# Token numbers of a mixture-of-experts layer copied out of the row buffers after the last convolution, and seven row buffers instead of eight

## The chip, the core and the metric

The kernel runs on one core of a Trainium2 chip. Its engines are PE (TensorE, matrix products), ACT (ScalarE, activations and copies out of PSUM), DVE (VectorE, elementwise work and reductions), POOL (GpSimd; here it issues the indirect DMAs above all) and SP (SyncE; here it only issues DMAs). The metric is the device time of one execution in microseconds (us). The median of three runs of the kernel before is 3093.45 us.

## The reference, cut to what matters

Input is x of 8 x 56 x 56 x 256 in float32, that is 25088 tokens of 256 channels. A convolution block of 32 parallel paths is followed by an attention step with a linear kernel and by a mixture of eight experts, each token taking the two that its router likes best. The last part is the one that the change touches:

```python
logits = tokens.astype(jnp.float32) @ router_w.astype(jnp.float32).T
probs = jax.nn.softmax(logits, axis=-1)
rw, re = jax.lax.top_k(probs, TOP_K)
...
for e in range(E):
    h = jax.nn.gelu(tokens @ w1[e] + b1[e], approximate=False)
    y = h @ w2[e] + b2[e]
    out = out + combine[:, e:e + 1] * y
```

The sum over the experts has only two terms a token that aren't zero. The kernel computes those two and adds each to the output row of its token.

## The kernel before, in words

**Slots.** The main loop runs over slots `s`. The input is cut into S = 56 chunks of 448 tokens (seven an image), and in slot `s` the convolution of chunk `s` runs together with the attention of chunk `s - 8` and with tiles of the experts' work whose tokens are already known. After slot 56 no convolution is left; slots 57 to 64 hold the last attention and routing and more tiles, and behind the loop come the remaining tiles.

**Routing.** For each group of chunks `route_steps` picks the two experts of every token, counts its place in each expert's list, and writes into the token's row three numbers behind its 256 channels: the two weights and, in column C + 2, the number of the token as an integer. POOL then scatters the rows into DRAM (`regions`, L1163), one region for the first choice (k = 0) and one for the second (k = 1), sorted by expert. When some chunks of an image are done, `plan_steps` (L1189) makes a plan of further tiles: for each, the first row in the region and the expert. There are 17 such plans, each of n tiles with k = 0 and then n tiles with k = 1; n tiles of one k are called a block here. All in all there are 210 tiles of 256 rows. The last plan holds tiles 176 to 192 (k = 0) and 193 to 209 (k = 1). Of each of its two blocks the first two tiles are surely full; the other fifteen can hold only part of their rows.

**One tile.** The steps of a tile `i` are spread over rounds. `moe_steps` (L1473) puts into round `n`:

1. `tile_in(n)`: PE turns the rows of tile n (L1375), ACT copies them out as `eT` (L1379); ahead of the next step one `tile_add`
2. `tile_mid(n - 1, 0)`: PE's first product with the expert's weights (L1415), ACT's gelu (L1419); one `tile_add`
3. `tile_mid(n - 1, 1)`, then `take_rows(n + 2)`: SP loads the 256 rows of tile n + 2 (L1354)
4. `tile_out(n - 2, 0)`: PE's second product (L1431, L1435), ACT's scaling by the router's weight into `y` (L1439); then `take_weights(n + 1)`: SP loads that tile's weights (L1364)
5. `tile_out(n - 2, 1)`

`tile_add` (L1444) issues on POOL an indirect DMA (L1453) that adds one half of y, 128 rows, to the output rows of its tokens. A tile has two such scatters. They take the token numbers as their index. `ordered_sum` (L1461) makes the scatters of a block wait until all those of the block before have landed, since two blocks can add to the same output rows; inside a block no row occurs twice.

**Buffers.** Row tiles (tag `rows`, 128 x 2 x 259 float32) have eight buffers, weights (`w`) four, `y` four of 128 x 2 x 256. A row buffer is read by PE (the turning), by ACT in `tile_out` (the router's weight, column C + k) and, in most tiles, by the scatters, whose index is the column C + 2 of the buffer itself. It is free when all these are done. In the thirty tiles that can be partly filled the index is already a buffer of its own: DVE makes it (L1386, L1387) from the column and from the number of the first valid row. These have 12 buffers of tag `index`.

**Order.** PE, ACT and DVE run their instructions in the order in which the program names them; the steps of a slot are placed by hand with the numbers in `places`. The instructions of SP and POOL are ordered by the compiler, from program order and from which buffers are free. [...] SP carries the loads of rows and weights, and also the loads and stores of the convolution and the attention (`tT` L958, `X` L959, the store of X L1034).

**A flag.** `apart` is an empty list until slot 57 and holds one element from then on (L1600). Up to now it only decides whether the two halves of a tile share one PSUM bank or have one each (`bank_of`). By the numbers in `places["after"]` and the plan, tile 129 is the first whose `tile_in` runs in slot 57.

**The start.** `empty_rows` (L1339) is called once in each of slots 1 to 8; it fills a buffer of tag `rows` with zeros and stores it into both regions.

Of the kernel before, what the change touches and what calls it, by code (L numbers as in the profile page):

```python
# [8 lines left out]
F32 = mybir.dt.float32  # L9
BF16 = mybir.dt.bfloat16  # L10
I32 = mybir.dt.int32
# [14 lines left out]
def kernel(  # L26
# [24 lines left out]
    nc = tc.nc  # L51
    B, N, C = x.shape
# [6 lines left out]
    P = 128  # L59
# [397 lines left out]
    slots = ctx.enter_context(tc.tile_pool(name="slots", bufs=4))  # L457
# [43 lines left out]
    ROW = C + 3  # L501
# [6 lines left out]
    def paced(ins):  # L508

        tc.add_manual_dep(ins, pace[0].name, SYNC, reason="spread over the slot")  # L510
        return ins
# [92 lines left out]
    def unordered(ins, group, keep=()):  # L604

        tc.declare_no_dep(ins, group=group, keep=keep, reason="other rows")
# [447 lines left out]
    def filled(b, ins):  # L1054
        unordered(ins, "rows")
        unordered(ins, "tiles")
        tc.add_to_no_dep_group("rows", ins)
        before.setdefault(b, []).append(ins)
# [266 lines left out]
    def entry(i, j, most):  # L1325

        place, own, k, partial, b = slot_of[i]
        loads, (value,) = nc.values_load_multi_w_load_instructions(
            place[0:1, j : j + 1], engines=[mybir.EngineType.SP],
            min_val=0, max_val=most,  # L1330
            skip_runtime_bounds_check_because="a tile's row and expert, made on the chip",
        )
        if b not in landed:
            landed.add(b)
            for ins in before[b]:
                tc.add_manual_dep(loads[0].ins, ins.name, SYNC, reason="rows of the tiles")
        return value

    def empty_rows(e):  # L1339
        pad = slots.tile([P, 2, ROW], F32, tag="rows", name=f"pad_{e}", bufs=8)  # L1340
        nc.gpsimd.memset(pad, 0.0)
        for k in range(2):
            ins = nc.sync.dma_start(
                out=regions[k][e * CAPR : e * CAPR + TR, :].rearrange("(h p) c -> p h c", p=P),
                in_=pad,
            ).ins
            paced(ins)
            filled(0, ins)

    def take_rows(i):  # L1350
        row = entry(i, 0, E * CAPR - TR)
        z = slots.tile([P, 2, ROW], F32, tag="rows", name=f"rows_{i}", bufs=8)
        region = regions[slot_of[i][2]]
        ins = nc.sync.dma_start(  # L1354
            out=z, in_=region[bass.ds(row, TR), :].rearrange("(h p) c -> p h c", p=P)
        ).ins
        unordered(ins, "rows")
        tc.add_to_no_dep_group("tiles", ins)
        got[i] = z
# [9 lines left out]
    def tile_in(i):  # L1369
        z = got.pop(i)  # L1370
        k = slot_of[i][2]
        tp = ps_mm.tile([P, NF, TR], F32, tag="mm", name=f"te_{i}")
        for f in range(NF):
            for h in range(2):
                nc.tensor.transpose(  # L1375
                    tp[:, f, h * P : (h + 1) * P], z[:, h, f * P : (f + 1) * P], ident
                )
        eT = work.tile([P, NF, TR], F32, tag="eT", name=f"eT_{i}")
        nc.scalar.copy(eT, tp)  # L1379
        g = z[:, :, C + k]  # L1380
        index = [z[:, h, C + 2 :].bitcast(I32) for h in range(2)]
        low = slot_of[i][3]
        if low is not None:
            index = slots.tile([P, 2], I32, tag="index", name=f"index_{i}", bufs=12)
            past = slots.tile([P, 2], I32, tag="past", name=f"past_{i}", bufs=2)
            nc.vector.tensor_scalar(past, pos, low, float(1 << 30), ALU.is_lt, ALU.mult)  # L1386
            nc.vector.tensor_tensor(  # L1387
                index, z[:, :, C + 2].bitcast(I32), past, ALU.bitwise_or
            )
            index = [index[:, h : h + 1] for h in range(2)]  # L1390
        turned[i] = (eT, g, index)

    apart = []
# [79 lines left out]
    def moe_steps(first, last):  # L1473


        steps = []

        def some(fn, i, *args):
            if 0 <= i < N_ALL:
                fn(i, *args)  # L1480

        for n in range(first, last):
            steps.append((0.5, lambda n=n: (some(tile_in, n), tile_add())))
            steps.append((1.0, lambda n=n: (some(tile_mid, n - 1, 0), tile_add())))
            steps.append((1.0, lambda n=n: (some(tile_mid, n - 1, 1), some(take_rows, n + 2))))
            steps.append((1.0, lambda n=n: (some(tile_out, n - 2, 0), some(take_weights, n + 1))))
            steps.append((1.0, lambda n=n: some(tile_out, n - 2, 1)))
        return steps
# [53 lines left out]
    for s in range(S + A + 1):  # L1542
# [53 lines left out]
        if 1 <= s <= E:  # L1596
            work_of.append((0.5, 0.5, [(0.0, lambda: copy_weights(s - 1))]))
            work_of.append((0.8, 0.8, [(0.0, lambda: empty_rows(s - 1))]))
# [65 lines left out]
```

## Time and profile before

| What | Value |
|---|---|
| median of three runs | 3093.45 us |
| lowest and highest run | 3087.57 and 3095.67 us |
| the profiled execution's own time | 3092.02 us |
| its span (first to last instruction) | 3090.3 us |
| mean granted clock of PE | 0.972 |
| PE busy | 2875.4 us, 93% |
| DVE busy | 2124.4 us, 69% |
| ACT busy | 1920.2 us, 62% |
| POOL busy | 1800.1 us, 58% |
| scatters that add y to the output (L1453, index in the row buffer) | 360, 1575 ns mean |
| scatters of rows into the regions (L1163) | 448, 957 ns mean |
| loads of rows, of weights | 210 each |

How to read it: busy times are sums over the whole span, and the stages differ. The convolution fills PE until slot 56; the expert tiles that the change touches run late, so what matters is read from the last 400 us, in the timelines of single engines and in busy times by stage. In a timeline each line has the start and the duration in us, the engine and line, the operation and its tiles, the number of merged instructions, and in brackets the idle time of the engine before it and what ended that. In a table of waits the three numbers are the total in us, how often, and the longest. In busy times by stage come first the stage and its length, then the busy time (and count) of PE, of PE's weight loads, of DVE, ACT and POOL, the granted clock, the DMA engines' busy share and GB/s. A wait for several semaphores is put down to the one that came last by the profile; an engine named there that had long been done was not what was waited for.

### The profile page before, as it was taken

The page shows a single profiled execution, that of the slowest core. Times are in us where ns is not written, and L with a number is a line of the kernel's source. Part 1 is how long each engine was busy: PE and PEld are TensorE (multiplying, and loading weights), DVE is VectorE, ACT ScalarE, POOL GpSimd, SP SyncE. Part 2 cuts the span into 40 slices and gives each one's busy share as a digit, 9 for nine tenths or more (in the row PEclk, how much of TensorE's full clock was granted, in tenths as well). Part 3 has the DMA queues.
Part 4 walks back from the last instruction along what each step waited for, and adds up shares of the span by engine and source line. Part 5 has one row for each costly group of instructions (what it writes and reads, how often), then busy time and mean ns, then how long its engine had stood idle before and what let it go on. Part 6 is the DMA issues. An engine that isn't in the chain of part 4 may idle for free.

```text
span 3090.3 us, 53454 instructions
## 1 busy us (share of the span) xinstructions
PE 2875.4 (93%) x16677; PEld 1645.2 (53%) x16677; DVE 2124.4 (69%) x5532; ACT 1920.2 (62%) x3859; POOL 1800.1 (58%) x1333
## 2 busy tenths in 40 slices
PE   7999898888999999999999999999999997997798
PEld 3334443433455555555555555555555554776687
DVE  6877778788777777787777777787778784544000
ACT  4666566556666666667766666666666764554355
POOL 2332344445465765756766666576664556676677
PEclk8999999889999999999999999999999999998899
DMA  3534344436456777677776776767766666998897
GB/s 101 151 118 129 115 141 134 129 98 198 140 158 185 186 193 188 177 198 190 193 193 164 197 197 171 200 168 199 198 171 175 184 169 157 228 254 201 201 236 172
DMA packets 321708, 537.53 MB, mean 174 GB/s; under 512 B 40192, under 2 KB 231824, under 8 KB 321424
## 3 DMA queue, kind: packets, MB, share of 16 engines
q1 hardware_dynamic: 238464, 429.89, 45.6%
q0 software_dynamic: 82368, 103.47, 18.6%
q8 instruction: 133, 2.18, 0.3%
q14 instruction: 151, 1.24, 0.1%
q10 hardware_dynamic: 592, 0.76, 0.1%
HBM read 248.01 MB, written 192.55 MB: 143 GB/s over the span
## 4 chain that ended last, share of the span: by engine, by line
PE 72%; DVE 8%; ACT 6%; POOL 5%; DMA 5%; issue 4%; SPq 0%; ACTq 0%; POOLq 0%; DVEq 0%
PE c L660 14%; PE su L681 13%; PE ph L1415 11%; PE py L1435 9%; PE at L983 7%; PE kv L829 3%; PE c L324 3%; ACT r L665 3%; POOL hsd L793 3%; PE te L1375 3%; PE c L288 2%; DVE r L668 2%; PE py L1431 2%; DMA w<-Wd 2%; DMA out_dram<-y,rows 2%
## 5 line engine op out<-in xcount | busy, mean ns | idle before, releaser
L668 DVE SCALAR_TENSOR_TENSOR r<-c,nb,r 128x448 f32<-128x448 f32 x1792 | 1128.3, 677 | 401.2 <-ACT r L665 395.5
L665 ACT ACTIVATE r<-c,b3t 128x448 f32<-128x448 f32 x1792 | 1036.6, 634 | 342.6 <-PE c L660 338.1
L1453 POOL DMA_INDIRECT out_dram<-y,rows x360 | 567.0, 1575 | 415.6 <-ACT y L1439 262.8
L660 PE MATMUL c<-hl,W3hl 64*128 64x448 f32 x3584 | 684.9, 427 | 32.5 <-ACT r L665 18.7
L1163 POOL DMA_INDIRECT regions<-pay,rrowi x448 | 428.5, 957 | 308.9 <-PE c L660 172.8
L660 PEld LDWEIGHTS c<-hl,W3hl 64*128 64x128 f32 x3584 | 324.3, 188 | 490.6 <-issue 207.7
L681 PE MATMUL su<-r,gather 128*32 128x448 f32 x3584 | 532.2, 564 | 36.3 <-DVE r L668 32.5
L1415 PE MATMUL ph<-eT,w 128*128 128x256 f32 x1680 | 454.5, 402 | 40.2 <-DMA w<-Wd 24.0
L1439 ACT ACTIVATE y<-py,rows 128x256 f32<-128x256 f32 x420 | 196.9, 473 | 442.0 <-PE py L1435 364.9
L1435 PE MATMUL py<-w,hT 128*128 128x256 f32 x1680 | 432.8, 382 | 0.0
L1415 PEld LDWEIGHTS ph<-eT,w 128*128 128x128 f32 x1680 | 301.2, 194 | 173.0 <-issue 45.8
L793 POOL TENSOR_TENSOR hsd<-hsd,half 112x36 f32<-112x36 f32 x49 | 302.7, 6178 | 88.0 <-DVE hsd L791 84.1
L754 POOL TENSOR_TENSOR norm<-t,hmean 112x512 f32<-112x512 f32 x112 | 115.5, 1057 | 361.0 <-DVE hmean L743 220.9
L1419 ACT ACTIVATE hT<-ph,w 128x256 f32<-128x256 f32 x420 | 198.1, 476 | 187.7 <-PE ph L1415 130.9
L1435 PEld LDWEIGHTS py<-w,hT 128*128 128x128 f32 x1680 | 292.1, 192 | 29.3
L983 PE MATMUL at<-tab,tT 128*112 128x272 f32 x896 | 258.2, 411 | 7.1 <-ACT r L665 5.9
L681 PEld LDWEIGHTS su<-r,gather 128*32 128x32 f32 x3584 | 97.2, 109 | 218.7 <-issue 101.7
L1431 PE MATMUL py<-b2hl,own 128*128 128x256 f32 x420 | 182.2, 434 | 11.6 <-ACT lg L991 7.8
L983 PEld LDWEIGHTS at<-tab,tT 128*112 128x112 f32 x896 | 148.3, 179 | 81.5 <-issue 27.7
L987 DVE SCALAR_TENSOR_TENSOR X<-at,rs,X 112x256 f32<-112x256 f32 x224 | 107.0, 478 | 107.2 <-PE at L983 106.6
L1431 PEld LDWEIGHTS py<-b2hl,own 128*128 128x128 f32 x420 | 80.5, 192 | 141.8 <-issue 48.0
L324 PE MATMUL c<-R,W2t 96*32 96x448 f32 x1344 | 149.3, 546 | 0.1
(263 smaller groups left out, 3063.1 us busy)
## 6 DMA issues: line engine op xcount, KB each, us to landing
w<-Wd SPq DMA_DIRECT2D x210, 513.0 KB
rows<-regions SPq DMA_DIRECT2D x210, 259.0 KB
xi<-in_x_dram SPq DMA_DIRECT2D x56, 448.0 KB
hl<-hi SPq DMA_DIRECT2D x112, 224.0 KB
tTs<-xT SPq DMA_DIRECT2D x56, 448.0 KB
ts<-t SPq DMA_DIRECT2D x56, 448.0 KB
tT<-tTs SPq DMA_DIRECT2D x56, 448.0 KB
X<-ts SPq DMA_DIRECT2D x56, 448.0 KB
```

Of the source, the lines that this page charges most:

```text
L324: nc.tensor.matmul(ps[0][32 * g : 32 * g + 32, :CH], W2t[:, g, dy, :], R[:, g, :].rearrange("q (r w) -> q r w", w=W58)[:, dy : dy + ROWS, ...
L660: product = nc.tensor.matmul(tiles[g][:, :CH], W3hl[rows, ab, cg, :], hl[rows, ab, :], start=True, stop=True)
L665: nc.scalar.activation(r, tiles[0][:, :CH], AF.Relu, bias=b3t[:, cg, 2 * ab : 2 * ab + 1])
L668: nc.vector.scalar_tensor_tensor(r, tiles[1][:, :CH], nb3[:, cg, 2 * ab + 1 : 2 * ab + 2], r, op0=ALU.max, op1=ALU.add,)
L681: nc.tensor.matmul(ps[32 * c4 : 32 * c4 + 32, :CH], gather, unit.pop((s, 4 * u + c4)), start=(ab == 0), stop=(ab == NQ - 1),)
L793: nc.gpsimd.tensor_tensor(sd, sd, half[:T, :].rearrange("q (k h) -> q k h", k=KT), ALU.pow)
L983: nc.tensor.matmul(ps, tT[:, f, k * T : (k + 1) * T], tables_of[b][:, f, :], start=(f == 0), stop=(f == NF - 1),)
L1163: ins = nc.gpsimd.indirect_dma_start(out=regions[n], out_offset=bass.IndirectOffsetOnAxis(ap=v["row_i"][:, (m - group[0]) * KT + k, n : n ...
L1415: nc.tensor.matmul(ps, w[:, f * C + hf * P : f * C + (hf + 1) * P], eT[:, f, :], start=(f == 0), stop=(f == NF - 1),)
L1431: nc.tensor.matmul(ps, own.to_broadcast([P, P]), b2hl, start=True, stop=False)
L1435: nc.tensor.matmul(ps, hT[:, f, h * P : (h + 1) * P], w[:, (NF + f) * C : (NF + f + 1) * C], start=False, stop=(f == NF - 1),)
L1453: ins = nc.gpsimd.indirect_dma_start(out=out_rows, out_offset=at, in_=y[:, h, :], in_offset=None, compute_op=ALU.add, **partial,).ins
```

## The change

In `tile_in` a tile whose index was the column of its row buffer gets an index buffer of its own, once `apart` holds an element: DVE copies the column's two integers a partition into a 128 x 2 tile of tag `index`, and the scatters read that. This is so for tiles 129 to 177, 193 and 194; the thirty partly filled tiles keep their own way of making an index. The tag has 20 buffers instead of 12. The tag `rows` has seven buffers instead of eight, in both places that use it, for the whole kernel.

```diff
     def empty_rows(e):
-        pad = slots.tile([P, 2, ROW], F32, tag="rows", name=f"pad_{e}", bufs=8)
+        pad = slots.tile([P, 2, ROW], F32, tag="rows", name=f"pad_{e}", bufs=7)
         nc.gpsimd.memset(pad, 0.0)
...
     def take_rows(i):
         row = entry(i, 0, E * CAPR - TR)
-        z = slots.tile([P, 2, ROW], F32, tag="rows", name=f"rows_{i}", bufs=8)
+        z = slots.tile([P, 2, ROW], F32, tag="rows", name=f"rows_{i}", bufs=7)
...
         index = [z[:, h, C + 2 :].bitcast(I32) for h in range(2)]
         low = slot_of[i][3]
-        if low is not None:
-            index = slots.tile([P, 2], I32, tag="index", name=f"index_{i}", bufs=12)
+        if apart and low is None:
+            index = slots.tile([P, 2], I32, tag="index", name=f"index_{i}", bufs=20)
+            nc.vector.tensor_copy(index, z[:, :, C + 2].bitcast(I32))
+            index = [index[:, h : h + 1] for h in range(2)]
+        elif low is not None:
+            index = slots.tile([P, 2], I32, tag="index", name=f"index_{i}", bufs=20)
             past = slots.tile([P, 2], I32, tag="past", name=f"past_{i}", bufs=2)
```

## The prediction

> **What bounds the kernel now.** I read the views in this order: the chain of waits, SP's queue and the engines' waits from 2600 us on, then the timelines of SP, ACT and POOL there, then busy time by stage. The change acts only there: the copies begin with tile 129, in the first slot without a convolution. Tiles are numbered by counting the records of a line (one row load, two y activations and two summing scatters a tile, 210 tiles).
>
> The lines that speak for the change come first: SP's queue, the engines' waits, and one moment on SP and on ACT.
>
> ```profile
> SPq L1354 <- DMA out_dram<-y,rows: 162.6, 41, 13.4
> ```
> ```profile
> ACT y L1439 <- DMA out_dram<-y,rows: 54.8, 13, 12.2
> ...
> PE ph L1415 <- DMA w<-Wd: 24.0, 16, 3.6
> ...
> PE te L1375 <- DMA rows<-regions: 8.6, 4, 7.5
> ```
> ```profile
> 2791.88 0.38 SPq L1354 DMA_DIRECT2D rows<-regions  x1
> 2792.88 0.33 SPq L1364 DMA_DIRECT2D w<-Wd  x1
> ```
> ```profile
> 2791.92 0.47 ACT L1439 ACTIVATE y<-py,rows 128x256 f32<-128x256 f32 x1 [12.15 <-DMA out_dram<-y,rows]
> ```
>
> SP stands 162.6 us at the row load until a scatter has landed, the weight load queues behind it, and PE then waits 24.0 us for weights and 8.6 us for rows. But one landing released both SP (2791.88) and ACT (2791.92). That is the buffer count: in round m the row load of tile m+2 needs, with eight buffers, the scatters of tile m-6; y of tile m-2, with four buffers, needs the same tile. So if SP's wait goes, ACT's stays. The question is what makes the scatters late: POOL.
>
> ```profile
> 2926.99 1.54 POOL L1453 DMA_INDIRECT out_dram<-y,rows  x1 [0.30 <-ACT y L1439]
> 2928.84 1.54 POOL L1453 DMA_INDIRECT out_dram<-y,rows  x1 [0.31 <-issue]
> 2935.00 1.54 POOL L1453 DMA_INDIRECT out_dram<-y,rows  x1 [4.62 <-ACT hT L1419]
> 2936.85 1.54 POOL L1453 DMA_INDIRECT out_dram<-y,rows  x1 [0.30 <-issue]
> ```
> ```profile
> 2922.39 0.84 ACT L1439 ACTIVATE y<-py,rows 128x256 f32<-128x256 f32 x2 [2.56 <-DMA out_dram<-y,rows]
> ```
> ```profile
> 2694.00:2834.00 140.00, 120.94 (x627) 103.09 (x626) 53.01 (x250) 72.70 (x176) 98.89 (x76) 0.94 0.91 233
> 2834.00:2955.00 121.00, 98.47 (x469) 83.10 (x468) 26.14 (x116) 50.92 (x115) 83.62 (x63) 0.90 0.85 205
> 2955.00:3091.00 136.00, 122.59 (x647) 107.85 (x646) 8.21 (x49) 72.03 (x148) 104.47 (x68) 0.97 0.82 201
> ```
> ```profile
> 3015.50 1.54 POOL L1453 DMA_INDIRECT out_dram<-y,index  x1 [0.30 <-issue]
> 3021.39 1.56 POOL L1453 DMA_INDIRECT out_dram<-y,rows  x1 [4.34 <-ACT y L1439]
> ...
> 3069.85 1.54 POOL L1453 DMA_INDIRECT out_dram<-y,index  x1 [0.69 <-ACT y L1439]
> ...
> 3073.98 1.54 POOL L1453 DMA_INDIRECT out_dram<-y,index  x1 [0.74 <-ACT y L1439]
> ...
> 3083.22 1.54 POOL L1453 DMA_INDIRECT out_dram<-y,index  x1 [0.30 <-issue]
> ```
>
> The scatter at 2935.00 is the first of tile 172. Its y was written from 2922.39 on, 12 us before, so POOL did not wait for PE or ACT. It is the first tile of a block, and its scatters wait until all of the block before have landed (L1461). Every idle time of POOL over 1 us after 2694.3 stands before a block's first tile: 7.17, 6.14, 5.35, 3.80, 6.16, 4.62, 5.03 and 4.34 us, at tiles 144, 149, 154, 165, 168, 172, 176 and 193. The rest is gapless: 207 instructions, 287.0 us busy (98.89 + 83.62 + 104.47), 207 x 0.30 = 62 us between them, eight long gaps 42.6 - 8 x 0.30 = 40 us, and 6 us after the last scatter: 395 of 397 us. **POOL alone fills the time from 2694 us to the end.** It waited for y only twice at the very end (0.69 and 0.74). The chain of waits names PE because in the last 130 us PE runs just as tight, started off by the same scatters.
>
> [...] 162.6 us stand at SP's row load, and the weight load at 2792.88 comes 1.0 us after it. [...] The summing scatters from 2694 us on land in 2.7 us at best and 5.4 at the median. [...] the trace has 160 ns for the like L1387. [...]
>
> **The change part by part**, against the profiled execution's 3092.02 us (span 3090.3).
>
> *SP's wait goes.* From tile 129 on a row buffer is free after the second y activation instead of after the landing. The load of tile i then waits for y of tile i-7, which needed the scatter of tile i-11: three tiles, 3 x 3.7 = 11 us of POOL's time, earlier than the i-8 of now. That covers most of the 13.4 us of the longest wait. PE's 24.0 + 8.6 us go, but PE then waits through ACT and the four y buffers for the same scatters. Hidden by POOL: 0. At the end PE, with a lead, brings y of tiles 206 and 207 in time: (0.69 - 0.30) + (0.74 - 0.30) = **-0.8 us**.
>
> *The gaps at block ends* are landing times[...]. Now SP fires rows and weights right after a landing, often into the next block's end; with the change they start earlier and more evenly. The trace already has a stretch that runs so, from tile 178 on, whose index lies apart: its one gap is 4.34 us. The seven before come to 38.3; at 4.34 each, 30.4, so 7.9 less. The other end is a burst at each block end, 7.17 us as at tile 144: 7 x 7.17 - 38.3 = 11.9 more. I take half the gain, **-4.0 us**, because one gap is thin evidence.
>
> *The copies.* 51 tiles (129 to 177, 193, 194) x 0.16 = 8.2 us of VectorE, busy 53.0 of 140 and 26.1 of 121 us there: 0. Without that cover a copy ahead of a routing step costs 0.16 us. A copy waits for its rows, and the attention's L987 and the routing queue behind it on VectorE; PE's transposes wait for the same rows at the same place, and the rows come earlier: 0. Its index buffer was last read 20 tiles, over 70 us, ago. [...] POOL's scatters take 1.54 us with VectorE all but idle (2955 on) and 1.55 with it busy.
>
> *Seven buffers instead of eight.* Up to tile 128 buffers are still held to the landing, so loads up to tile 135 wait for the scatters of tile i-7. With 5.5 us for a landing, no load before tile 127 is touched. That of tile 127 goes from 2599.80 to about 2612 (tile 120's second scatter is issued at 2606.73, behind 15 scatters of rows on POOL). Behind it on SP stands the attention's load L958, which went at 2612.79 anyway. Tiles 128, 129, 134 and 135 slip 1 to 5 us, and PE takes each over 10 us later. Cost 0; if the landing of tile 120 took 15 us instead of 5.5, up to 10. The pads of the start (L1339) are loaded hundreds of us earlier: 0.
>
> *Sum:* 3092.0 - 0.8 - 4.0 = 3087.2. The median of the runs shown is 1.4 us above the profiled execution, so 3088.6; I write 3088.
>
> **The rivals.** *PE sets the end.* The chain of waits gives PE 72% and runs through scatter, weight load and L1415. If PE's stalls were the limit, its 24.0 us for weights would go: 3092.0 - 24.0 = 3068 (3059 with the 8.6 for rows). Against it: POOL's 395 of 397 us. For it: POOL's and SP's orders are not written out by hand, so a new order could lay other scatters into the gaps, as at tiles 158 and 162 now. *Slower: prefetch into the block ends.* Weights and rows that run ahead are under way when a block's last scatter is to land, and the gaps grow to 7.17 us: 3092.0 - 0.8 + 11.9 = 3103. It decides from (9.3 + 0.8) / 7 = 1.4 us a gap. Against it: PE stalls in those gaps, and SP's weight load waits for PE. *The change does nothing*, because y of the same tile holds the row buffer: 3092, inside the forecast.
>
> **How the numbers follow.** Forecast 0.72, PE sets the end 0.16, slower 0.12. A measurement tells about 0.3% here, 9.3 us, from no change. The forecast's own range is 3080 to 3097, and about 0.11 of its chance lies more than 9.3 us under 3093.45; so faster 0.27, same 0.61, slower 0.12. The range 3070 to 3098 leaves out the slower case and the lower half of the faster one, 0.2 together.
>
> **What would show it.** Right: SP's 162.6 us at the row load nearly gone, PE's waits for weights a few us, ACT's wait for scatters still there or larger, POOL gapless from about 2694 us on but for the block ends, with gaps near 5 us. Wrong: POOL waiting for y in the middle of blocks, another order on POOL that fills the gaps, gaps over 7 us, or rows of tiles 127 to 135 late for PE.

## The result and the profile after

In twenty runs each, taken beside one another, the changed kernel has a median of 3085.57 us (3080.62 to 3093.95) and the kernel before one of 3095.32 us. The ratio is 0.9974, with a 95% interval of 0.9967 to 0.9981: 8.0 us less of 3095, between 6 and 10; the two medians themselves lie 9.8 us apart. The forecast was 4.8 us less.

The profiled execution of the changed kernel took 3093.95 us (span 3092.1) and is the longest of its twenty. Its convolution alone ends 7.9 us later than before's (the last activation at L665 starts at 2582.0 us, before at 2574.1), at a lower granted clock (0.967 over the span, before 0.972), and of the change only the seven buffers act up to there. So spans are not compared here. The stretch compared is the one that the prediction spoke of: from the first scatter of tile 135 (2694.3 us before, 2701.7 after) to the start of the last scatter.

First SP's queue from 2600 us on, then the engines' waits there (total in us, how often, longest):

```profile
SPq L1364 <- PE py L1439: 200.8, 74, 12.3
...
SPq L1354 <- DMA out_dram<-y,rows: 19.1, 4, 10.7
SPq L1354 <- ACT y L1443: 14.4, 7, 6.5
```
```profile
ACT y L1443 <- DMA out_dram<-y,index: 79.4, 18, 11.7
POOL out_dram L1457 <- ACT y L1443: 43.1, 35, 6.4
...
PEld te L1375 <- ACT y L1443: 23.6, 5, 7.6
PE te L1375 <- ACT y L1443: 21.9, 4, 7.2
```

The change does what it says. SP's wait at the row load for a landing falls from 162.6 to 19.1 us, and what is left of it lies ahead of 2720 us, at tiles whose buffers were still held to a landing. SP itself stands nearly as long as before: it now waits 200.8 us at the weight load until PE is done with a weight buffer (84.6 before). The lines "PE ph <- DMA w" (24.0 us before) and "PE te <- DMA rows" (8.6 us) are gone. And the wait has moved as foretold: ACT now stands 79.4 us for the four y buffers (54.8 + 2.1 before), and PE's transposes stand 21.9 us behind ACT's y. PE lost one wait and got another, which leads through ACT to the landing of scatters.

POOL is nearly as gapless as it was. Its timeline at the starts of the blocks of tiles 168, 172 and 193, and near the end:

```profile
2910.76 1.54 POOL L1457 DMA_INDIRECT out_dram<-y,index  x1 [0.31 <-issue]
2917.57 1.54 POOL L1457 DMA_INDIRECT out_dram<-y,index  x1 [5.26 <-ACT y L1443]
...
2930.51 1.54 POOL L1457 DMA_INDIRECT out_dram<-y,index  x1 [0.30 <-ACT hT L1423]
2935.43 1.54 POOL L1457 DMA_INDIRECT out_dram<-y,index  x1 [3.38 <-ACT hT L1423]
...
3016.86 1.54 POOL L1457 DMA_INDIRECT out_dram<-y,index  x1 [0.30 <-ACT hT L1423]
3020.51 1.56 POOL L1457 DMA_INDIRECT out_dram<-y,index  x1 [2.11 <-ACT hT L1423]
...
3067.53 1.54 POOL L1457 DMA_INDIRECT out_dram<-y,index  x1 [0.74 <-ACT y L1443]
...
3071.66 1.54 POOL L1457 DMA_INDIRECT out_dram<-y,index  x1 [0.74 <-ACT y L1443]
...
3085.03 1.54 POOL L1457 DMA_INDIRECT out_dram<-y,index  x1 [0.31 <-issue]
```

Tile 168 waits 5.26 us (6.16 before), tile 172 3.38 (4.62), tile 193 2.11 (4.34). The 0.74 at the end is new in number: it stands at eight tiles, where before 0.69 and 0.74 stood at two.

Every kernel of this study can be read in that way. The columns: the stretch; the waits before the eight blocks, summed; what other waits of POOL take beyond the usual 0.30 us between two instructions; and the rest, that is the first less the other two.

| Kernel (chip) | Stretch | Eight block waits | Other waits | Rest |
|---|---|---|---|---|
| before (first) | 388.9 | 42.6 | 0.8 | 345.5 |
| changed (first) | 383.3 | 34.8 | 3.6 | 344.9 |
| before_again (second) | 397.8 | 38.9 | 14.7 | 344.3 |
| change_again (second) | 390.7 | 39.1 | 7.5 | 344.2 |
| change_third (second) | 393.8 | 39.0 | 10.0 | 344.8 |
| seven_alone (second) | 402.9 | 37.5 | 20.4 | 345.0 |
| copies_eight (second) | 389.8 | 37.4 | 7.4 | 345.0 |
| weights_first (second) | 392.3 | 34.7 | 12.4 | 345.2 |
| split_before (second) | 384.0 | 7.8 | 31.0 | 345.2 |
| split_after (second) | 380.3 | 5.6 | 30.7 | 344.1 |
| y_five (third) | 383.1 | 38.7 | 0 | 344.5 |
| one_weights (third) | 379.8 | 34.8 | 0 | 345.0 |
| alternate (third) | 362.8 | 18.7 | 0 | 344.2 |
| alternate_y5 (third) | 362.5 | 18.0 | 0 | 344.5 |

The rest is POOL's own work: scatters of 1.54 and 0.95 us with 0.30 between them. It is 344 to 345.5 us in all fourteen, whatever PE, SP and the buffers do. That work plus waits is the stretch holds for any queue by the way of counting. What the table adds is that the work is the same everywhere, so that two stretches differ by POOL's waits alone. Whether a wait is POOL's own (for a landing that its own scatters must wait for) or one for a late y of PE and ACT, the columns tell: in the kernel before, all waits for y come to 0.8 us, on the first chip. So the 5.6 us from before to after are -7.8 in the block waits, +2.8 in waits for y at the end and -0.6 in the rest. That is one profile of each kernel; where the other 2 to 4 us between the medians lie, no profile shows.

### The profile page after: what moved, and what is told of

Its sections match the earlier page's. It is cut to its first block, busy times and chain, and to the rows that moved or that the text cites. A ratio compares the mean times of both kernels' runs of the same rounds, so it can differ in the third digit from the quotient of the medians.

```text
span 3092.1 us, 53582 instructions
## 1 busy us (share of the span) xinstructions
PE 2883.2 (93%) x16677; PEld 1650.4 (53%) x16677; DVE 2127.7 (69%) x5583; ACT 1917.2 (62%) x3859; POOL 1799.2 (58%) x1333
## 4 chain that ended last, share of the span: by engine, by line
PE 58%; DVE 6%; POOL 4%; ACT 3%; issue 3%; DMA 3%; POOLq 0%; ACTq 0%; DVEq 0%; SPq 0%
PE ph L1419 11%; PE c L660 10%; PE py L1439 9%; PE su L681 9%; PE at L983 6%; PE te L1375 3%; PE kv L829 2%; PE py L1435 2%; PE c L324 2%; DMA out_dram<-y,index 2%; POOL hsd L793 2%; DVE r L668 2%; ACT r L665 1%; PE c L288 1%; POOL out_dram L1457 1%
## 5 line engine op out<-in xcount | busy, mean ns | idle before, releaser
L665 ACT ACTIVATE r<-c,b3t 128x448 f32<-128x448 f32 x1792 | 1036.6, 634 | 349.2 <-PE c L660 344.8
L1457 POOL DMA_INDIRECT out_dram<-y,rows x258 | 407.8, 1580 | 332.6 <-ACT y L1443 246.2
L1419 PE MATMUL ph<-eT,w 128*128 128x256 f32 x1680 | 453.3, 401 | 16.2 <-ACT hT L1423 10.6
L1457 POOL DMA_INDIRECT out_dram<-y,index x162 | 251.6, 1553 | 96.2 <-ACT y L1443 41.7
```

The costliest lines, as they stand in the source:

```text
L665: nc.scalar.activation(r, tiles[0][:, :CH], AF.Relu, bias=b3t[:, cg, 2 * ab : 2 * ab + 1])
L1419: nc.tensor.matmul(ps, w[:, f * C + hf * P : f * C + (hf + 1) * P], eT[:, f, :], start=(f == 0), stop=(f == NF - 1),)
L1457: ins = nc.gpsimd.indirect_dma_start(out=out_rows, out_offset=at, in_=y[:, h, :], in_offset=None, compute_op=ALU.add, **partial,).ins
```

## The experiments

Theory: POOL's queue sets the length of the last 390 us, and what isn't a wait of POOL costs nothing. First rival: PE's waits for weights (24.0 us), which SP's standing caused, were the limit. Second: SP's traffic sets the block waits. The runs lie on two further chips. On each the kernel before was run beside them, and every ratio is against it there (medians 3106.61 and 3107.36 us on the second, 3091.39 on the third).

**The two parts of the change, one at a time.** `change_again` is the changed kernel on the second chip.

> The changed kernel once more, for a second profile. POOL theory (from about 2694 us on POOL's queue sets the end; the change acts only by shorter idle times of POOL at the ends of blocks, and hands some back at the very end to PE): 6 to 10 us faster than before; the seven long idle times of POOL from tile 144 to 176 come to 30 to 34 us in place of 38.3, and POOL waits for y in the last ten tiles. Weights theory (SP's wait at the row load delayed PE's weights, and that was the cost): same time, but POOL's idle times stay near 38 us.

Measured: 3108.59 us, 1.0005 (0.9994 to 1.0017). The 6 to 10 us that the theory foresaw are not there, and neither are shorter block waits (39.1 us). `change_third` and `before_again`, the same two kernels once more with other runs, tell chance from the chip:

> The kernel before once more, for a profile on the chip of these runs. Within 2 us of itself. If the loss of the gain on the second chip is the chip's own (PE and ACT standing without a cause that the profile names, at 2609 and 2741 us of the changed kernel there), this profile shows the same stops and POOL waiting for y; if not, POOL's queue is gapless from 2694 us on but for the ends of blocks, as in the first profile.

> The changed kernel a third time. POOL theory: where PE keeps its lead, 6 to 10 us faster than before, from shorter idle times at the ends of blocks; where PE or ACT stops for another reason and POOL waits for y in the middle of blocks, within 3 us of before. Weights theory: 6 to 10 us faster everywhere, since SP's wait goes everywhere.

Measured: 1.0003 (0.9995 to 1.0012) for the unchanged kernel and 1.0004 (0.9992 to 1.0016) for the changed one. On this chip the change moves nothing that can be told in the time. The profile shows a difference between the chips: ACT and PE stand for some us where the trace names no cause, and then POOL, which waited for y only at the very end on the first chip, does so inside blocks. From `before_again`, ACT and then POOL:

```profile
2735.19 0.59 ACT L1379 COPY eT<-te 128x512 f32<-128x512 f32 x1 [6.19 <-remote]
```
```profile
2741.36 1.55 POOL L1453 DMA_INDIRECT out_dram<-y,rows  x1 [3.12 <-ACT y L1439]
...
2756.12 1.55 POOL L1453 DMA_INDIRECT out_dram<-y,rows  x1 [2.52 <-ACT y L1439]
...
2768.79 1.55 POOL L1453 DMA_INDIRECT out_dram<-y,rows  x1 [4.85 <-ACT y L1439]
```

The last line is the block start of tile 144; the two ahead of it stand inside a block. "remote" means that the trace knows no releaser. Such waits come to 17.8 us at ACT's hT and 13.2 at its eT in `before_again` from 2690 us on; in the profiles of the first and third chip no such line is among the sixty largest waits from 2600 us on. Why the second chip has them was not found, but it can be said where it is slower. The span of `before_again` is 18.0 us longer than that of the first chip's profile of the same kernel: 2.7 us up to the last activation of the convolution, 6.4 from there to tile 135, 8.9 in the stretch.

The change does act on this chip too. In `before_again` POOL waits 15 times for y after 3000 us, 6.1 us in all; in `change_again` and `change_third` never, and their stretches are 7.1 and 4.0 us shorter. The stage from the convolution to tile 135 is 1.8 us longer in both, and the medians show no gain. So here a difference of some us between single profiles is not one of the medians, and where the rest went stays open.

`seven_alone` takes only the seven buffers, in both places, without the copies; the place of the loads:

```diff
-        z = slots.tile([P, 2, ROW], F32, tag="rows", name=f"rows_{i}", bufs=8)
+        z = slots.tile([P, 2, ROW], F32, tag="rows", name=f"rows_{i}", bufs=7)
```

> The kernel before with seven row buffers and no copies. Row loads then wait for the scatters of tile i-7, one tile tighter than y's four buffers. POOL theory: SP waits longer, PE's waits for weights about double, and POOL is starved at some blocks: 5 to 15 us slower than before. Weights theory: PE's waits for weights and rows, 33 us before, double and all of it counts: 25 to 35 us slower. If only the loads of tiles 127 to 135 suffered: within 3 us.

Measured: 3117.45 us, 1.0032 (1.0023 to 1.0042), 10 us slower than before. Its profiled execution is the longest of its runs, so only its stretch is read. It is 5.1 us longer than in `before_again`, which is half of the 10: the other waits are 20.4 us against 14.7, and PE stands longer for weights (12.5 us against 7.4):

```profile
POOL out_dram L1453 <- ACT y L1439: 45.5, 42, 6.6
...
PE ph L1415 <- DMA w<-Wd: 12.5, 7, 3.0
```

With seven buffers held until the landing, a row load needs the scatters of a tile that POOL issues one tile later than with eight. That this puts PE behind POOL fits these waits; where the other 5 us lie is open. `copies_eight` takes only the copies, with eight row buffers and 12 index buffers as before:

```diff
-        if low is not None:
+        if apart and low is None:
+            index = slots.tile([P, 2], I32, tag="index", name=f"index_{i}", bufs=12)
+            nc.vector.tensor_copy(index, z[:, :, C + 2].bitcast(I32))
+            index = [index[:, h : h + 1] for h in range(2)]
+        elif low is not None:
```

> The copies with eight row buffers, and 12 index buffers as before so that all fits. POOL theory: the eighth buffer is worth nothing, within 3 us of the change (6 to 10 us faster than before). If the seven buffers cost time in the slots before tile 129 (loads of tiles 127 to 135): 3 to 10 us faster than the change.

Measured: 3111.47 us, 1.0014 (1.0005 to 1.0022), beside 1.0005 (0.9994 to 1.0017) for the whole change. It lies within 3 us of `change_again`, as the theory has it, but it is not 6 to 10 us faster than before: it is some 4 us slower, by an interval that leaves out no change, and its profile, the shortest of its runs, does not say why. With the copies the eighth buffer brings no gain that can be told. Without them it is worth 10 us.

**PE's weights without the change.** `weights_first` is the kernel before with the two loads of a round swapped, so that SP's stand at the row load (up to 13.4 us in the first profile of before, where the weight load of 2792.88 us went 1.00 us after the row load) no longer holds up the weights.

```diff
-            steps.append((1.0, lambda n=n: (some(tile_mid, n - 1, 1), some(take_rows, n + 2))))
-            steps.append((1.0, lambda n=n: (some(tile_out, n - 2, 0), some(take_weights, n + 1))))
+            steps.append((1.0, lambda n=n: (some(tile_mid, n - 1, 1), some(take_weights, n + 1))))
+            steps.append((1.0, lambda n=n: (some(tile_out, n - 2, 0), some(take_rows, n + 2))))
```

> The kernel before, with each round's weight load placed ahead of its row load, so that no weight load queues behind the row load's wait. Weights theory: PE's 24 us of waits for weights go, and with them most of the change's gain comes, 6 to 10 us faster. POOL theory: PE's waits for weights go, the end hardly moves: 0 to 4 us faster.

Measured: 3108.00 us, 1.0001 (0.9988 to 1.0013). PE's largest wait for loads from 2600 us on, in `before_again` and then here:

```profile
PE ph L1415 <- DMA w<-Wd: 7.4, 4, 3.0
```
```profile
PE te L1375 <- DMA rows<-regions: 8.4, 6, 2.7
```

The line "PE ph <- DMA w" is gone here; a wait for rows has taken its place, and the time has not moved. On this chip the wait for weights was only 7.4 us, not 24.0; as a price by itself it would make the ratio 1 - 7.4 / 3107 = 0.9976, and the interval excludes that. But PE stands as long as before for loads (9.5 us in `before_again` from 2694 us on, 8.4 here), so a rival that holds all standing of PE to be the price is not touched by this run. Two other things speak against it. In the kernel before on the first chip, with its 24.0 us, POOL waited for y only 0.8 us, so PE brought nearly every y in time. And in `y_five` below PE waits for no load at all and POOL for no y, and the block waits are there as ever. The first rival falls as the limit of the stretch.

**The block waits.** If POOL's waits cost their full length, taking away the ordering between the two blocks of a plan shows how much room there is. In `split_before` (the kernel before) and `split_after` (the changed one) the k = 1 tiles are summed into a second array, so that their sum doesn't reach the output (the result is no longer whole), and a block waits only for the last one of the same k:

```diff
+    second = tc.dram_tile([NTOK, C], F32, name="second")
...
-            out=out_rows, out_offset=at, in_=y[:, h, :], in_offset=None,
+            out=second if slot_of[i][2] else out_rows,
+            out_offset=at, in_=y[:, h, :], in_offset=None,
...
-        before_it = blocks.get((b, 0) if k else (b - 1, 1), [])
+        before_it = blocks.get((b - 1, k), [])
```

> The kernel before, with the scatters of the second choice (k = 1) summed into a scratch tensor instead of the output, so that a block waits only for the block of the same k one plan earlier, whose scatters landed long ago. The sum of the second choices is left out of the output. POOL theory: POOL's eight long idle times (42.6 us) go and PE sets the end: 20 to 32 us faster than before. Weights theory: POOL is not the limit, within 4 us of before.

> The same edit in the changed kernel; the sum of the second choices is left out of the output. POOL theory: 20 to 35 us faster than the changed kernel, and the lead over the split kernel before is smaller than 5 us, since without late scatters SP's wait at the row load shrinks by itself. Weights theory: within 4 us of the changed kernel.

Measured: 3098.07 us, 0.9968 (0.9953 to 0.9983), and 3097.39 us, 0.9972 (0.9961 to 0.9983). That is some 9 to 10 us, not the 20 and more that were expected. The block waits fell by 38.9 - 7.8 = 31.1 us against `before_again`; the other waits rose by 31.0 - 14.7 = 16.3. The stretch is 13.8 us shorter, the median 10.6 below that of `before_again`. Where the gain went can be seen on POOL in `split_before`:

```profile
2937.02 1.54 POOL L1454 DMA_INDIRECT second<-y,rows  x1 [0.30 <-issue]
...
2944.87 1.54 POOL L1454 DMA_INDIRECT second<-y,rows  x1 [0.62 <-ACT y L1440]
2946.72 1.54 POOL L1454 DMA_INDIRECT second<-y,rows  x1 [0.31 <-DMA rows<-regions]
2949.00 1.54 POOL L1454 DMA_INDIRECT second<-y,rows  x1 [0.73 <-ACT y L1440]
2950.84 1.54 POOL L1454 DMA_INDIRECT second<-y,rows  x1 [0.30 <-DMA rows<-regions]
2953.12 1.54 POOL L1454 DMA_INDIRECT out_dram<-y,rows  x1 [0.74 <-ACT y L1440]
```

The block starts at 2937.02 without a wait; within three tiles each tile's first scatter waits 0.73 or 0.74 us for y. A tile then takes 4.13 us (2944.87, 2949.00), while two scatters take 2 x 1.85 = 3.70. 4.13 us is PE's pace. The busy times of that time in `split_before` show PE busy without a break, and DVE, ACT and POOL not:

```profile
2945.00:3080.00 135.00, 135.00 (x723) 119.84 (x721) 9.43 (x57) 81.45 (x164) 101.38 (x66) 1.00 0.94 231
```

The same 4.13 us stand at the end of the kernel before and of the changed one. PE was next to set the end, and far closer than I had taken. `split_after` is within 1 us of `split_before`; since on this chip the change is worth nothing with the block waits either, that says no more.

`alternate` keeps the whole result. In the changed kernel every second plan runs its k = 1 tiles first. A plan then begins with the k with which the last one ended, and two blocks of the same k have no row in common, so no ordering is needed there. A block waits for the opposite k: a plan's first for that of the two plans before, its second for that of its own plan and the one before.

```diff
-                slot_of[2 * first + k * n + i] = (
+                slot_of[2 * first + (k ^ b % 2) * n + i] = (
...
-        before_it = blocks.get((b, 0) if k else (b - 1, 1), [])
+        other = (b, b - 1) if k ^ b % 2 else (b - 1, b - 2)
+        before_it = sum((blocks.get((o, 1 - k), []) for o in other), [])
```

> The changed kernel with the two blocks of every second plan in the other order (first k = 1, then k = 0). Neighbouring blocks of two plans then have the same k, share no output row and need no wait, so four of the eight long idle times of POOL go (before tiles 144, 154, 168 and 176, some 22 us), and the result is whole. POOL theory, with PE next in line about 10 us behind as the split kernels showed: 4 to 10 us faster than the changed kernel. Weights theory: within 3 us of the changed kernel.

Measured: 3071.69 us, 0.9933 (0.9918 to 0.9949). POOL at the starts of the blocks of tiles 168, 172 and 176:

```profile
2894.27 1.54 POOL L1457 DMA_INDIRECT out_dram<-y,index  x1 [0.30 <-ACT eT L1379]
2896.12 1.54 POOL L1457 DMA_INDIRECT out_dram<-y,index  x1 [0.31 <-issue]
...
2909.05 1.54 POOL L1457 DMA_INDIRECT out_dram<-y,index  x1 [0.30 <-issue]
2916.63 1.54 POOL L1457 DMA_INDIRECT out_dram<-y,index  x1 [6.03 <-ACT y L1443]
...
2929.56 1.54 POOL L1457 DMA_INDIRECT out_dram<-y,index  x1 [0.30 <-ACT y L1443]
2931.41 1.54 POOL L1457 DMA_INDIRECT out_dram<-y,index  x1 [0.30 <-issue]
```

Tiles 168 (2896.12) and 176 (2931.41) start with no wait; tile 172 keeps its own, for it follows the other k. Four of the eight waits are gone, and the other waits of POOL are 0. It is 20.7 us faster than before, where 4 to 10 us were expected over the changed kernel: that PE would follow 10 us behind was carried over from the second chip, and here POOL never waits for PE.

**A fifth y buffer.** If ACT's wait for y buffers (79.4 us) cost time of itself, a fifth would help. `y_five` is the changed kernel with five y buffers, and six row buffers to make room; `alternate_y5` is both edits.

```diff
-            hidden[i].append(work.tile([P, 2, C], F32, tag="y", name=f"y_{i}", bufs=4))
+            hidden[i].append(work.tile([P, 2, C], F32, tag="y", name=f"y_{i}", bufs=5))
```

> The changed kernel with five y buffers and six row buffers. POOL theory: the idle times of POOL stay, PE's lead grows by a tile and POOL waits less for y: 0 to 4 us faster than the changed kernel, unless the row loads before tile 129 suffer from six buffers (then up to 5 us slower). If ACT's wait for y buffers is the limit by itself: 8 us or more faster.

> Both edits together, the result whole. POOL theory: the gain of the other order plus 0 to 4 us, since PE is then the limit and no longer stands still at the ends of blocks: 6 to 14 us faster than the changed kernel.

Measured: 3089.75 us, 0.9993 (0.9980 to 1.0005), and 3067.08 us, 0.9918 (0.9903 to 0.9933). POOL never waits for y in `y_five`, as foreseen for the end, yet its block waits are 38.7 us. `alternate_y5` against `y_five` is the cleanest test of the sum, for the two lie on one chip and differ in the order of blocks alone: block waits 38.7 - 18.0 = 20.7 us less, stretch 20.6 less, median 22.7 less. So a block wait of POOL costs its full length where PE keeps up. `alternate_y5` is the lowest of all, 25 us under the kernel before it was run beside, but its stretch is that of `alternate` (362.5 and 362.8) and the intervals overlap: that the fifth buffer adds anything is not shown.

**Traffic and landings.** `one_weights` is the changed kernel with no weights loaded after tile 129; all later tiles multiply with that tile's weights, so the result is another.

```diff
+        if i > 129:
+            weights_of[i] = weights_of[129]
+            return
```

> The changed kernel without the weight loads after tile 129: all later tiles use that tile's weights, so their result is another. POOL theory (the idle times at block ends are landing times [...]): with 513 of about 1280 KB a tile gone, the eight idle times shrink from about 5 us each to 2 to 4, and the kernel is 5 to 12 us faster than the changed kernel. If traffic does not set the landing times, they stay at 5 us and the time stays within 3 us.

Measured: 3084.55 us, 0.9979 (0.9970 to 0.9987). Busy time from 2694 to 3080 us, the changed kernel (first chip) and then this one (third); the last two numbers are the DMA engines' busy share and GB/s:

```profile
2694.00:3080.00 386.00, 347.38 (x1773) 300.20 (x1772) 97.10 (x486) 195.43 (x445) 283.90 (x205) 0.94 0.91 226
```
```profile
2694.00:3080.00 386.00, 337.20 (x1734) 288.94 (x1733) 90.26 (x452) 184.99 (x434) 285.54 (x206) 0.95 0.65 121
```

The traffic falls from 226 to 121 GB/s and the eight block waits are 34.8 us in both. They are spread otherwise, 3.23 to 5.49 us instead of 2.11 to 6.39. The two profiles are of different chips, though, and the changed kernel itself was not run on the third. It has 39.1 and 39.0 us on the second chip, and `y_five`, its next of kin on the third, has 38.7. So without weight traffic the sum is 0 to 4 us lower, not the 8 to 24 us lower that waits of 2 to 4 us in place of about 5 would have given. Weight traffic is not what most of a block wait consists of; a share of the size of the forecast's 4.0 us is neither shown nor excluded.

## Why the prediction was right, and where it was not

**SP's wait going: 0.** Right on the first chip. The wait went (162.6 to 19.1 us), PE's waits for weights and rows went with it, ACT's wait for y took their place, and POOL had waited for y only 0.8 us, so there was nothing to win. On the second chip, where PE was late now and then, 6.1 us of POOL's waits for y went with it, though the medians show no gain.

**At the end: -0.8 us. Wrong in sign on the first chip.** The step said that PE, with a lead, brings y of tiles 206 and 207 in time. Measured is +2.8: eight tiles wait 0.44 us more than usual instead of two. On the second chip these waits went, as the step has it. In the first chip's profile the y buffers keep PE's lead short:

```profile
2965.08 0.84 ACT L1443 ACTIVATE y<-py,rows 128x256 f32<-128x256 f32 x2 [8.09 <-DMA out_dram<-y,index]
```

This is y of tile 180. It had to wait for the landing of tile 176, the first of its block, and POOL itself reached tile 180 eight scatters after tile 176, at 2955.87 + 8 x 1.85 = 2970.7. So PE's lead is some 5 us there. If it then loses 4.13 - 3.70 = 0.43 us a tile to POOL, as at the end, it wins back only what POOL waits at tile 193. That wait was 4.34 us before and is 2.11 now, and I take it that the 2.2 us won there come back as most of the 2.8 in front of the end. I had booked the two as separate terms. This is argued from one profile: in `copies_eight` tile 193 waits 2.93 us and no tile waits at the end, so more than this wait decides.

**Block ends: -4.0 us (-7.9 to +11.9).** On the first chip the likeliest sign was right and the size too small: the one pair of profiles has -7.8, namely 38.3 - 32.7 = 5.6 at the first seven and 2.2 at the eighth. That these waits are shorter when SP's rows and weights start earlier was my estimate, from one wait of 4.34 us beside seven of 38.3 us in sum; no run here shows that a landing grows by SP's loads. `one_weights` takes nearly half of the traffic away (226 to 121 GB/s), and the block waits are 0 to 4 us shorter in sum. So the estimate is not confirmed, and what made them shorter on the first chip is open: the moment at which SP's loads fall, a changed order, and the place of each block's last scatter in PE's pace are not excluded. Each chip has only one or two profiles of a kernel, and on the second the waits are 39.0 and 39.1 us with the change and 38.9 without. That the forecast came out as near as it did owes something to luck: the term that it rests on was half of what one wait of 4.34 us suggested, and its range, 3070 to 3098 us, holds no change at all as well.

**Copies: 0.** A copy took 0.16 us (median of 51), as costed, and the rest of POOL's stretch is 344.9 us with them and 345.5 without, so they did not slow POOL's scatters in any amount that can be seen. Against a plain 0 stands `copies_eight`, 4 us slower than before for a reason that is not known.

**Seven buffers: 0, up to 10.** Right for the change as a whole (`copies_eight`, with eight, is no faster). Alone they cost 10 us, which the text did not price, since it had the copies from tile 129 on.

**The rivals.** PE as the bound (3068) does not describe the kernel before on the first chip: POOL waited for its y only 0.8 us in the stretch, and the measured 3085.57 is far from 3068. But I had it too far off: in `split_before`, on the second chip, PE sets the pace once the block waits are gone, after a gain of 9 to 10 us. Of the slower case nothing was seen: no block wait of any profile with the change is over 7 us (the longest is 6.92, in `change_again`).

So the main step was right: one queue holds the end, and what the change does upstream of it is hidden as long as y comes in time. The 8 us are not what the change is built for. By the one pair of profiles they come from the block waits, for a reason that stays open. They came on the first chip and not on the second; on the third the changed kernel was not run by itself.

## What to carry to other kernels

A long wait in a table is a price only for the engine whose queue has no slack: here SP's wait at the row load fell by 143.5 us and the time by 8. Find that queue by adding up, in the stretch that ends last, its instructions, the short spaces between them and its waits: when it hardly waits for the other engines, as POOL here with 345 us of work, 43 of waits for its own landings and 1 of waits for y in 389, only its work and its own waits count, and a wait that is taken away from another engine can turn up again at the next buffer, as it did here. Then ask of such a queue's waits whether they need be at all: the order in which blocks follow one another was worth some 20 us, and the change of buffers 8 or nothing.

## What the runs showed of the hardware

The waits for the landings of eight blocks' last scatters hardly got shorter when the traffic beside them nearly halved (226 to 121 GB/s): 34.8 us in sum, against 34.8 to 39.1 in three profiles of the changed kernel and one of `y_five`. And the same two kernels differed by 0.26% on one chip and by nothing that can be told on another, where ACT stood up to 6.2 us in a place without a cause that the trace shows (`before_again`); a gain of this size holds for the chip on which it was measured.
